# Layer 1's experts: from every expert over all tokens to 23 gathered tiles of one expert each

## Chip, core and metric

The kernel is one program on one core of a Trainium2 chip. The metric is the device time of one execution in microseconds (us), as the median of several runs. Before the change it is 3067.04 us over 3 runs (3048.27 to 3077.75).

## What is computed

The program runs four layers over the same activations `x`, of which the kernel handles two batches of 1024 tokens with 128 channels, all in f32. Each layer normalises `x`, sends the result both through an attention part (giving `s`) and through a feed-forward part (giving `g` before a silu), and adds `s * silu(g)` to `x`. The change is in the feed-forward part of the second layer ("layer 1"), a mixture of eight experts of which each token uses two:

```python
probs = softmax(einsum('bsd,ed->bse', x, Wr))          # 8 experts
topv, topi = top_k(probs, 2)
combine = sum(topv[..., None] * one_hot(topi, 8), axis=2)
for w1, bb1, w2, bb2, ce in experts:                    # w1 128x512, w2 512x128
    h = gelu(x @ w1 + bb1, approximate=False)
    acc = acc + ce[..., None] * (h @ w2 + bb2)
```

An expert that a token did not choose has weight zero in the sum, so the reference's value is the same whether that expert's product is computed for the token or not.

## The kernel before

**How the program is built.** Each layer's two parts are Python generators that write instructions and `yield` now and then. `weave` (L423) interleaves them: in every turn a stream gets its rate added, and it advances one yield for each whole unit. `program` (L1712) calls it for layer 1 with the attention of both batches as one stream at rate 1 and the feed-forward of both batches, one after the other, as a second stream at rate `R1[1]` = 0.125: one feed-forward yield in eight attention yields. When the attention stream is used up, the feed-forward stream goes on alone. The order on each engine is fixed when the program is built. Position in the program is the priority; an instruction that is taken to be ready may be placed ahead of an earlier one that is not, so pieces of one stream also slip into gaps of the other. [...]

**Buffers.** Most data lie in one pool of 33 buffers of 128 x 1048 f32 (`half` and `arr`; `NHALF`), some in eight buffers of 128 x 512 (`t512`). PSUM has four banks for general use (`bank`) and two double banks (`bank2`). The weights of a layer have one buffer for the attention part (`wa`) and one for the feed-forward part (`wf`), which the next layer's weights reuse.

**Layer 1's attention** (`l1_attn`, L768). For each batch, four groups of four heads; for each group 16 rounds of a key tile by a query half. A round is four score products `sim` (into the two double banks), two exponentials `e` of 128x1024 on ACT (L882; each result takes a pool buffer), and the four products `av` of the round before, which accumulate in two of the four general banks over the whole group. One round is one yield; a group has 18 yields, so the two batches have 144. At the end of a batch its output is transposed and projected (`wt`, `pj`).

**Layer 1's feed-forward** (`l1_ffn`, L932). For each batch: eight small router products, a softmax and the rank of every expert for each token on DVE (L942 to L953), the combine weights `comb` (L955), the transposes of these and the product with `b2` that starts the sum `g`; one yield. Then 16 steps, for each expert and each half of 512 tokens: four `up` products (weights 128x128, 512 token columns), a Gelu on ACT from each of them (L977), 16 `down` products (128 tokens by 128 outputs each, four accumulated per token tile), and four DVE instructions that weight the result and add it to `g` (L988); one yield. A batch has 17 yields. `up` weights lie in `wf` (`w1`, 4096 columns), `down` weights in four pool buffers that are loaded ahead of the layer (`w2`, from `f1b`).

After both streams, `step` (L1734 to L1736) applies silu to `g`, multiplies by `s` and adds to `x`, and the next layer normalises `x`.

The trace has two matmul records for each f32 product of the code, one for a transpose. All products have the line of the helper `mm` (L335), all transposes L339; they are told apart by the name of the tile that they write.

Of the kernel before, what the change touches and what calls it, by code (L numbers as in the profile page):

```python
# [16 lines left out]
F32 = mybir.dt.float32  # L17
I32 = mybir.dt.int32
AF = mybir.ActivationFunctionType
ALU = mybir.AluOpType  # L20
X = mybir.AxisListType.X
PSUM = bass.MemoryType.PSUM

P = 128
NB = 2
L = 1024
T = NB * L
NT = T // P
TB = L // P
BLK = 512  # L30
NB2 = L // BLK
# [11 lines left out]
def _cols(v):  # L43

    v = np.asarray(v).reshape(-1)
    n = -(-v.size // P)
    out = np.zeros((n * P,), v.dtype)
    out[: v.size] = v
    return out.reshape(n, P).T


def _chunks(w):

    w = np.asarray(w)
    n = -(-w.shape[0] // P)
    out = np.zeros((n * P, w.shape[1]), w.dtype)
    out[: w.shape[0]] = w
    return out.reshape(n, P, w.shape[1]).transpose(1, 0, 2).reshape(P, -1)
# [12 lines left out]
def _pad(w):  # L71
    w = np.asarray(w)
    out = np.zeros((P, w.shape[1]), w.dtype)
    out[: w.shape[0]] = w
    return out


def _gains(q, k):
# [45 lines left out]
    ],  # L124
    "f1": [
        ("wr", 8, lambda i: i["L1_ffn_Wr"].T),
        ("b1", 32, lambda i: _cols(i["L1_ffn_b1"])),
        ("b2", 128, lambda i: _pad(i["L1_ffn_b2"])),
        ("w1", 4096, lambda i: i["L1_ffn_W1"].transpose(1, 0, 2).reshape(P, -1)),
    ],  # L130
    "a2": [
        ("wk", 1024, lambda i: i["L2_attn_Wk"].reshape(P, -1)),
# [37 lines left out]
        for l in range(2)  # L170
    },
    "f0b": [("h2", 2048, lambda i: _chunks(i["L0_ffn_h2_w"].T))],
    "f1b": [("w2", 4096, lambda i: _chunks(i["L1_ffn_W2"].reshape(-1, P)))],
}


def _constants():

    p = np.arange(P)[:, None]
    c = np.arange(P)[None, :]  # L180
    s = np.arange(192)[None, :]
    one = np.float32(1)
    strict = (c[:, :32] < p % 32) * one
    incl = (p % 32 <= c[:, :32]) * one
    return {
        "ident": (p == c) * one,
        "bo32": (p // 32 == c // 32) * one,
        "strict32": strict,
        "incl32": incl,
        "pad32": ((p // 32 == c[:, :32] % 4) & (p % 32 < 8)) * one,  # L190
        "quad4": (p // 32 == c[:, :4]) * one,
        "row8": (p % 32 == 8) * one,
        "bo64": (p // 64 == c // 64) * one,
        "upper": (p <= c) * one,
        "center": (p == c) * one - one / P,
        "mean": one / P + 0 * (p + c),


        "window": np.concatenate([np.where((s >= p) & (s <= p + 64), 0, -1e30)[:, o:] for o in (128, 0, 0)], axis=1),

        "every2": (c[:, :33] % 2 == 0) * one + 0 * p,
        "every4": (c[:, :35] % 4 == 0) * one + 0 * p,

        "turns": (p // 64 == c[:, :32] % 2) * one,

        "spread": np.concatenate([(p == 32 * (h % 4) + h // 4) * one + 0 * c[:, :64] for h in range(16)], axis=1),

        "spread2": (p % 32 == c // 64) * one,
        "ones": one + 0 * p + 0 * c,
        "head8": (p // 8 == c[:, :16]) * one,  # L210
        "slot": np.where(c < 127, c, -1) + 0 * p,
        "inv4": one / np.float32(10000) ** (np.arange(0, 8, 2, dtype=np.float32) / 8) + 0 * p,
    }


def _rotary():


    f = np.float32
    half = np.arange(0, 64, 2, dtype=f)  # L220
    t = np.arange(L, dtype=f)
    freqs = t[:, None] * (f(1) / f(10000) ** (half / f(64)))[None, :]
    power = (t - f(L // 2)) / f(32)
    scale = ((half + f(0.4 * 64)) / f(1.4 * 64))[None, :] ** power[:, None]
    cos, sin = np.cos(freqs), np.sin(freqs)
    both = [np.concatenate([sign * v, v], axis=1)
            for sign, v in ((1, cos * scale), (1, cos / scale), (-1, sin * scale), (-1, sin / scale))]
    tab = np.concatenate(both, axis=1).astype(f)
    return tab.reshape(TB, P, 256).transpose(1, 0, 2).reshape(P, -1)
# [14 lines left out]
def pack_inputs(inputs):  # L244
    out = {"x": np.ascontiguousarray(inputs["L0_attn_hidden_states"])}
    for name, spec in PACKS.items():
        out[name] = _pack(spec, inputs)
    out["bkv2"] = np.concatenate([np.reshape(inputs[f"L2_attn_b{n}"], (1, -1)) for n in "kv"], axis=1)
    out["mask2"] = np.ascontiguousarray(inputs["L2_ffn_attention_mask"][:NB, 0])

    pos = np.asarray(inputs["L2_ffn_position_ids"])[:NB]
    pos = np.pad(pos, ((0, 0), (0, L - pos.shape[1])), mode="edge")
    out["pos2"] = np.ascontiguousarray(pos.reshape(NT, P).T)

    out["stair"] = (np.arange(2 * L - P)[None, :] - (L - P) < np.arange(P)[:, None]).astype(np.float32)
    out["rotary"] = _rotary()
    out["const"] = np.ascontiguousarray(
        np.concatenate([v.astype(np.float32) for v in _constants().values()], axis=1)
    )
    return out  # L260
# [149 lines left out]
def tiles(v):  # L410
    return v.rearrange("p (t d) -> p t d", d=P)


def cols(t, n=1, w=P):
    return slice(t * w, (t + n) * w)


R0 = (20, 0.3)
R1 = (1, 0.125)
R2 = (1, 0.2, 0.2)  # L420


# [506 lines left out]
    C.project(out["s"], wT, w["wp"], w["bp"])  # L929


def l1_ffn(C, w, xnT, out):  # L932

    nc = C.nc
    E = 8
    n = TB * E
    ps = C.bank("router")
    for t in range(TB):
        C.mm(ps[:, t * E : (t + 1) * E], xnT[:, cols(t)], w["wr"])
    bye = lambda v: v.rearrange("p (t e) -> p t e", e=E)  # L940
    prob = bye(C.small("prob", n))
    nc.vector.tensor_copy(prob, bye(ps[:, :n]))  # L942
    C.softmax(prob, TB, E)

    rank = bye(C.small("rank", n))
    nc.gpsimd.memset(rank, 0.0)
    for f in range(E):
        pf = prob[:, :, f : f + 1]
        for lo, hi, op in ((0, f, ALU.is_gt), (f + 1, E, ALU.is_ge)):
            if lo < hi:  # L950
                c = C.small("cmp", TB * (hi - lo)).rearrange("p (t e) -> p t e", t=TB)
                nc.vector.tensor_tensor(c, pf.to_broadcast([P, TB, hi - lo]), prob[:, :, lo:hi], op)
                nc.vector.tensor_add(rank[:, :, lo:hi], rank[:, :, lo:hi], c)  # L953
    comb = bye(C.small("comb", n))
    nc.vector.scalar_tensor_tensor(comb, rank, 1.5, prob, ALU.is_lt, ALU.mult)  # L955

    acc, cT = C.arr("g"), C.arr("cT")
    for g in range(NB2):
        ps = C.bank("tr")
        for k in range(4):  # L960
            C.transpose(ps[:E, cols(k)], comb[:, 4 * g + k, :])
        C.evac(cT[:E, cols(g, 1, BLK)], ps[:E])
    for g in range(NB2):
        ps = C.bank("b2")
        for k in range(4):
            C.mm(ps[:, cols(k)], cT[:E, cols(4 * g + k)], w["b2"][:E])
        C.evac(acc[:, cols(g, 1, BLK)], ps)
    yield

    for e in range(E):  # L970
        for i in range(NB2):
            hh = [C.arr(f"h{a}") for a in range(2)]
            h = [hh[c // 2][:, cols(c % 2, 1, BLK)] for c in range(4)]
            for c in range(4):
                ps = C.bank("up")
                C.mm(ps, w["w1"][:, e * 512 + c * P : e * 512 + (c + 1) * P], xnT[:, cols(i, 1, BLK)])
                nc.scalar.activation(h[c], ps, AF.Gelu, bias=w["b1"][:, 4 * e + c : 4 * e + c + 1])  # L977
            ps = C.bank("down")
            for k in range(4):
                for c in range(4):  # L980
                    C.mm(
                        ps[:, cols(k)], h[c][:, cols(k)], w["w2"][e // 2][:, cols(4 * (e % 2) + c)],
                        start=c == 0, stop=c == 3,
                    )
            for k in range(4):
                t = 4 * i + k
                a = acc[:, cols(t)]
                nc.vector.scalar_tensor_tensor(a, ps[:, cols(k)], comb[:, t, e : e + 1], a, ALU.mult, ALU.add)  # L988
            yield
    out["g"] = acc  # L990


# [719 lines left out]
def program(tc, ins, out):  # L1712
    with ExitStack() as es:
        C = Ctx(es, tc, ins)
        nc = C.nc
        tokens = lambda d, b: d[b].rearrange("(t p) d -> p t d", p=P)
        x = []
# [24 lines left out]
        def layer(attn, ffn, rates):  # L1742
# [8 lines left out]
        wa, wf = C.weights("a0", "wa"), C.weights("f0", "wf")  # L1751
# [3 lines left out]
            lambda a, f: weave((a[0], 1), (a[1], 1, R0[0]), (chain(*f), R0[1])),  # L1755
        )
        wa, wf = C.weights("a1", "wa"), C.weights("f1", "wf")
        wf["w2"] = [C.loaded(f"w2_{i}", ins["f1b"][:, cols(i, 1, L)]) for i in range(4)]
        layer(
            lambda x, b, r: l1_attn(C, wa, x[1], r), lambda x, b, r: l1_ffn(C, wf, x[1], r),  # L1760
            lambda a, f: weave((chain(*a), R1[0]), (chain(*f), R1[1])),
        )
        wa, wf = C.weights("a2", "wa"), C.weights("f2", "wf")
# [5 lines left out]
        s = l3_attn(C, C.weights("a3", "wa"), xns)  # L1769
# [27 lines left out]
```

## Time and profile before

| | |
|---|---|
| Median of 3 runs | 3067.04 us |
| The profiled execution: its time / its span | 3056.8 us / 3055.0 us |
| Busy over the span: PE, DVE, ACT, POOL | 83%, 43%, 39%, 14% |
| Layer 1: from its first score products to the last sum into `g` | about 667 to 1436 us |
| In 690 to 1310 us (620 us): PE, DVE, ACT, POOL busy | 583.0, 92.6, 400.9, 4.9 us |
| In 1310 to 1440 us (130 us): PE, DVE, ACT, POOL busy | 121.3, 27.1, 53.5, 0.1 us |
| Share of the chain that ended last: PE, DVE, ACT | 62%, 19%, 10% |
| Indirect transfers, or other transfers issued by POOL | none in the program |

An engine's line shows how long its instructions ran. A row of groups or of the timeline has the line of the code, the engine, the tile written and the tiles read, the number of records, and the idle time before them with what ended it. PE records are pipelined and overlap each other: what a product costs is read from the distance between starts, not from a record's length. "Windows" gives each engine's busy time in a stretch of the span.

### The profile page before, as it was taken

The page shows a single profiled execution, that of the slowest core. Times are in us where ns is not written, and L with a number is a line of the kernel's source. Part 1 is how long each engine was busy: PE and PEld are TensorE (multiplying, and loading weights), DVE is VectorE, ACT ScalarE, POOL GpSimd, SP SyncE. Part 2 cuts the span into 40 slices and gives each one's busy share as a digit, 9 for nine tenths or more (in the row PEclk, how much of TensorE's full clock was granted, in tenths as well). Part 3 has the DMA queues.
Part 4 walks back from the last instruction along what each step waited for, and adds up shares of the span by engine and source line. Part 5 has one row for each costly group of instructions (what it writes and reads, how often), then busy time and mean ns, then how long its engine had stood idle before and what let it go on. Part 6 is the DMA issues. An engine that isn't in the chain of part 4 may idle for free.

```text
span 3055.0 us, 32385 instructions
## 1 busy us (share of the span) xinstructions
PE 2547.6 (83%) x13394; PEld 1288.6 (42%) x13394; DVE 1311.4 (43%) x2114; ACT 1180.4 (39%) x1488; POOL 417.9 (14%) x444
## 2 busy tenths in 40 slices
PE   6788975779999999997679687689989968878887
PEld 3445543433333333365335353433334335544554
DVE  4767577342101111023774655431122046566564
ACT  3300112245676766634111212353444424444443
POOL 0000102100000000000111110021111144343330
PEclk8866766788999999999778877799999978999998
DMA  2000000010000000001110000000000000000000
GB/s 85 19 21 15 1 0 1 11 57 1 1 1 1 1 1 1 1 29 57 52 56 21 1 0 24 17 1 1 1 1 1 8 31 1 8 8 1 4 4 8
DMA packets 33941, 41.78 MB, mean 14 GB/s; under 512 B 19969, under 2 KB 24833, under 8 KB 33665
## 3 DMA queue, kind: packets, MB, share of 16 engines
q1 hardware_dynamic: 33792, 39.70, 4.1%
q8 instruction: 105, 1.72, 0.2%
q14 instruction: 44, 0.35, 0.0%
HBM read 36.54 MB, written 3.15 MB: 13 GB/s over the span
## 4 chain that ended last, share of the span: by engine, by line
PE 62%; DVE 19%; ACT 10%; issue 4%; POOL 3%; SPq 1%; DMA 1%; POOLq 0%; ACTq 0%; DVEq 0%
PE sim L335 11%; PE num L335 6%; PE down L335 4%; PE av L335 4%; PE tr L339 3%; PE up L335 3%; PE z L335 3%; PE wo L335 3%; PE nd L335 3%; PE ph L335 2%; PE qk L335 2%; PE step L335 2%; PE spread L335 1%; PE hs L335 1%; PE pu L335 1%
## 5 line engine op out<-in xcount | busy, mean ns | idle before, releaser
L882 ACT ACTIVATE e<-sim 128x1024 f32<-128x1024 f32 x256 | 250.2, 1021 | 139.7 <-PE sim L335 139.4
L335 PE MATMUL sim<-q,k 32*128 32x512 f32 x1024 | 254.1, 674 | 4.4 <-ACT e L882 3.9
L988 DVE SCALAR_TENSOR_TENSOR g<-down,comb,g 128x128 f32<-128x128 f32 x128 | 36.0, 344 | 430.3 <-PE down L335 430.3
L1388 ACT ACTIVATE e<-sim 128x1024 f32<-128x1024 f32 (+1 forms) x192 | 146.8, 809 | 175.0 <-PE sim L335 174.8
L335 PE MATMUL num<-e,v 128*64 128x512 f32 (+4 forms) x1280 | 196.5, 429 | 0.9 <-POOL e L1390 0.9
L335 PE MATMUL sim<-q,kT 64*128 64x512 f32 (+3 forms) x768 | 159.5, 522 | 23.7 <-ACT sq L1348 14.2
L1390 POOL TENSOR_TENSOR e<-e,const 128x256 f32<-128x256 f32 x128 | 85.5, 680 | 530.1 <-ACT e L1388 526.5
L335 PE MATMUL av<-e,va 128*32 128x512 f32 x1024 | 156.8, 633 | 0.0
L332 DVE COPY q<-num 128x512 f32<-128x512 f32 x16 | 11.1, 691 | 323.7 <-PE num L335 323.7
L335 PEld LDWEIGHTS down<-w,h 128*128 128x128 f32 x1024 | 123.5, 193 | 48.9 <-ACT h L977 37.7
L335 PEld LDWEIGHTS sim<-q,k 32*128 32x128 f32 x1024 | 77.2, 193 | 158.2 <-ACT e L882 131.3
L335 PE MATMUL down<-w,h 128*128 128x128 f32 x1024 | 130.3, 280 | 9.0 <-ACT h L977 8.9
L335 PE MATMUL z<-e,const 128*32 128x192 f32 (+5 forms) x1344 | 130.6, 415 | 1.6 <-ACT e L1597 1.6
L335 PE MATMUL up<-xnT,w_f 128*128 128x512 f32 x256 | 123.9, 609 | 2.1 <-ACT h L977 2.0
L1542 POOL TENSOR_TENSOR sq<-qk,tab 128x256 f32<-128x256 f32 x128 | 97.2, 791 | 206.9 <-DVE ss L1531 191.4
L335 PEld LDWEIGHTS num<-e,v 128*64 128x64 f32 x1280 | 81.2, 137 | 94.0 <-issue 72.3
L335 PEld LDWEIGHTS sim<-q,kT 64*128 64x128 f32 x768 | 62.5, 188 | 131.3 <-issue 71.3
L977 ACT ACTIVATE h<-up,w_f 128x512 f32<-128x512 f32 x128 | 85.2, 686 | 72.9 <-PE up L335 71.2
L1014 POOL TENSOR_SCALAR e<-e 128x512 f32<-128x512 f32 x32 | 48.2, 1510 | 302.3 <-ACT e L1013 295.2
L339 PE MATMUL tr<-const,u 128*128 128x128 f32 x384 | 60.8, 316 | 33.7 <-DVE u L1550 29.3
L600 DVE SCALAR_TENSOR_TENSOR conv<-vT,w_a,conv 128x1024 f32<-128x1024 f32 x60 | 81.3, 1355 | 1.4
L335 PE MATMUL g<-z,w_f 128*128 128x512 f32 (+1 forms) x48 | 36.4, 851 | 53.3 <-DVE z L1656 53.3
(506 smaller groups left out, 4572.3 us busy)
## 6 DMA issues: line engine op xcount, KB each, us to landing
stair<-in_stair SPq DMA_DIRECT2D x16, 512.0 KB, 3.6
w_f<-in_f SPq DMA_DIRECT2D x14, 512.0 KB, 5.0
w_a<-in_a SPq DMA_DIRECT2D x8, 512.0 KB, 4.5
w<-in_f1b SPq DMA_DIRECT2D x4, 512.0 KB, 7.5
mk<-in_mask SPq DMA_DIRECT2D x4, 512.0 KB, 5.1
tab<-in_rotary SPq DMA_DIRECT2D x4, 512.0 KB, 3.8
const<-in_const SPq DMA_DIRECT2D x1, 1422.5 KB, 6.0
x<-in_x SPq DMA_DIRECT2D x2, 512.0 KB, 8.0
```

The costliest lines, as they stand in the source:

```text
L332: self.nc.vector.tensor_copy(dst, src)
L335: self.nc.tensor.matmul(out, lhsT=lhsT, rhs=rhs, start=start, stop=stop, **k)
L339: self.nc.tensor.transpose(out, in_, self.ident[:n, :n])
L600: nc.vector.scalar_tensor_tensor(av, vT[:, f + t : f + t + L], cw[:, t : t + 1], av, ALU.mult, ALU.add)
L882: nc.scalar.activation(es[jj], ps[jj].rearrange("p i n -> p (i n)"), AF.Exp)
L977: nc.scalar.activation(h[c], ps, AF.Gelu, bias=w["b1"][:, 4 * e + c : 4 * e + c + 1])
L988: nc.vector.scalar_tensor_tensor(a, ps[:, cols(k)], comb[:, t, e : e + 1], a, ALU.mult, ALU.add)
L1014: nc.gpsimd.tensor_scalar_min(e, e, 1.0)
L1388: nc.scalar.activation(e[:, :, :n], ps[:, :, :n], AF.Exp, scale=16.0)
L1390: nc.gpsimd.tensor_tensor(e[:, :, :P], e[:, :, :P], C.c["upper"].unsqueeze(1).to_broadcast([P, 2, P]), ALU.mult)
L1542: nc.gpsimd.tensor_tensor(t4[:, j, :, a], c4[:, j, :, z], sin, ALU.mult)
```

## The change

The feed-forward part of layer 1 computes each token only with its two experts. A batch has 2048 pairs of token and expert; sorted by expert, with each expert's block filled up to a multiple of 128, they fit into at most 23 tiles of 128 slots whatever the routing, and the program always runs 23. DVE and small products find the slot of each pair, then for each slot its token and weight, and for each tile its expert. POOL issues indirect transfers ("gathers", one row of DRAM per partition by an index in SBUF): per tile one for the 128 tokens (from a copy `xd` of the normalised activations in DRAM) and one for the expert's weights (from a new input `experts`, 1028 f32 to a row: `w1`, `w2` and the bias); and 16 per batch to collect the results by slot from a DRAM copy `yd`. The tiles run in six sets of up to four with a yield after each. The bias is added by a DVE instruction ahead of the Gelu instead of by the Gelu itself. The `b2` product is moved to the end. `w1`, `b1` leave the `f1` pack and the four `w2` loads go. Rate `R1[1]` is 0.2 instead of 0.125.

```diff
-R1 = (1, 0.125)
+R1 = (1, 0.2)
...
-def l1_ffn(C, w, xnT, out):
+def l1_ffn(C, w, xn, xnT, b, out):
...
+    NTILE = (2 * L + E * (P - 1)) // P
+    xd = C.dram.tile([L, P], F32, tag=f"xd{b}", name="xd")
+    nc.sync.dma_start(out=xd.rearrange("(t p) d -> p t d", p=P), in_=tiles(xn))
...
+    yield
+    sel, comb = bye(C.small("sel", n)), bye(C.small("comb", n))
+    nc.vector.tensor_single_scalar(sel, rank, 1.5, ALU.is_lt)
+    nc.vector.tensor_mul(comb, sel, prob)
+    before = C.t512("before")[:, : (TB + 1) * E].rearrange("p (t e) -> p t e", e=E)
+    nc.gpsimd.memset(before[:, 0], 0.0)
+    for t in range(TB):
+        nc.vector.tensor_add(before[:, t + 1], before[:, t], sel[:, t])
+    ps = C.bank("place")
+    C.mm(ps[:, :n], C.c["upper"], sel.rearrange("p t e -> p (t e)"), stop=False)
+    C.mm(ps[:, :n], C.c["ones"], before[:, :TB].rearrange("p t e -> p (t e)"), start=False)
+    C.mm(ps[:, n : n + E], C.c["ones"], before[:, TB])
+    yield
...
+    slots = C.sml.tile([P, 2 * TB], I32, tag="slots", name="slots", bufs=2)
+    nc.vector.tensor_copy(slots, slot)
+    yield
+    rows = [C.arr(f"rows{k}") for k in range(2)]
+    for k in range(2):
+        nc.vector.tensor_tensor(
+            tiles(rows[k]), C.c["count"].unsqueeze(1).to_broadcast([P, TB, P]), over(row[:, k * TB : (k + 1) * TB], P),
+            ALU.is_equal,
+        )
...
+    ps = C.bank("fill")
+    for a in range(2 * TB):
+        C.mm(
+            ps[:, : 2 * NTILE], rows[a // TB][:, cols(a % TB)], put[:, a].rearrange("p s j -> p (s j)"),
+            start=a == 0, stop=a == 2 * TB - 1,
+        )
+    token = C.sml.tile([P, NTILE], I32, tag="token", name="token", bufs=2)
...
+    expert = C.sml.tile([P, NTILE], I32, tag="expert", name="expert", bufs=2)
+    nc.vector.tensor_copy(expert, owner)
+    yield
+    def gather(dst, src, index):
+        nc.gpsimd.indirect_dma_start(
+            out=dst, out_offset=None, in_=src, in_offset=bass.IndirectOffsetOnAxis(ap=index, axis=0)
+        )
+    yd = C.dram.tile([NTILE * P, P], F32, tag=f"yd{b}", name="yd")
+    for j0 in range(0, NTILE, 4):
+        js = range(j0, min(j0 + 4, NTILE))
+        m = len(js) * P
+        xg, y = C.t512("xg"), C.t512("y")
+        for j in js:
+            gather(xg[:, cols(j - j0)], xd, token[:, j : j + 1])
+        ps = C.bank("tr")
+        for j in js:
+            C.transpose(ps[:, cols(j - j0)], xg[:, cols(j - j0)])
+        xT = C.t512("xT")
+        nc.vector.tensor_copy(xT[:, :m], ps[:, :m])
+        hs, ws = [], []
+        for j in js:
+            we = C.half("we")[:, : 2 * 512 + 4]
+            gather(we, C.ins["experts"], expert[:, j : j + 1])
+            ps = C.bank("up")
+            for c in range(4):
+                C.mm(ps[:, cols(c)], we[:, cols(c)], xT[:, cols(j - j0)])
+            h = C.t512("h")
+            nc.vector.tensor_tensor(tiles(h), tiles(ps), over(we[:, 1024:], P), ALU.add)
+            nc.scalar.activation(h, h, AF.Gelu)
+            hs.append(h)
+            ws.append(we)
+        ps = C.bank("down")
+        for j, h, we in zip(js, hs, ws):
+            for c in range(4):
+                C.mm(ps[:, cols(j - j0)], h[:, cols(c)], we[:, 512 + c * P : 512 + (c + 1) * P], start=c == 0, stop=c == 3)
+        nc.vector.tensor_tensor(
+            tiles(y[:, :m]), tiles(ps[:, :m]), over(weight[:, j0 : j0 + len(js)], P), ALU.mult
+        )
+        nc.sync.dma_start(out=yd[j0 * P : j0 * P + m].rearrange("(t p) d -> p t d", p=P), in_=tiles(y[:, :m]))
+        yield
     acc, cT = C.arr("g"), C.arr("cT")
...
-    for e in range(E):
-        for i in range(NB2):
-            hh = [C.arr(f"h{a}") for a in range(2)]
...
-            yield
+    for k in range(2):
+        y = C.arr(f"y{k}")
+        for t in range(TB):
+            gather(y[:, cols(t)], yd, slots[:, k * TB + t : k * TB + t + 1])
+        nc.vector.tensor_add(acc, acc, y)
+        yield
     out["g"] = acc
...
-        wf["w2"] = [C.loaded(f"w2_{i}", ins["f1b"][:, cols(i, 1, L)]) for i in range(4)]
```

## The prediction

> **What bounds the kernel now.** I read the page for the busiest engine and the chain that ended last, then windows over layer 1, then chain and timeline inside it. PE is the busiest engine of the kernel and carries the chain. Windows of layer 1 (columns: us, then busy time and records of PE, PE weight loads, DVE, ACT, POOL, then granted clock), first the stretch with both streams, then the one in which the experts run alone:
>
> ```profile
> PE 62%; DVE 19%; ACT 10%; issue 4%; POOL 3%; SPq 1%; DMA 1%; POOLq 0%; ACTq 0%; DVEq 0%
> ```
>
> ```profile
> 690.00:1310.00 620.00, 582.98 (x2942) 217.61 (x2941) 92.61 (x323) 400.93 (x436) 4.86 (x9) 0.95 0.00 1
> 1310.00:1440.00 130.00, 121.32 (x673) 89.73 (x672) 27.13 (x75) 53.45 (x74) 0.11 (x1) 0.96 0.12 40
> ```
>
> PE is at 94% and 93%. POOL does nothing. Is PE the bound of attention alone, too? Windows over six attention rounds without an expert step (16.01 us), and over eight rounds with one expert step (31.88 us):
>
> ```profile
> 858.04:874.05 16.01, 15.90 (x99) 4.41 (x97) 0.17 (x1) 11.71 (x13) 0.00 (x0) 1.00 0.01 2
> 858.04:889.92 31.88, 31.11 (x180) 11.15 (x177) 1.30 (x5) 24.46 (x26) 0.00 (x0) 1.00 0.00 1
> ```
>
> A round takes 16.01/6 = 2.67 us, PE busy 99%, ACT 73%. An expert step among them takes 31.88 - 8 x 2.67 = 10.5 us. The PE timeline of the tail shows what such a step is when alone:
>
> ```profile
> 1409.35 2.74 PE L335 MATMUL up<-xnT,w_f 128*128 128x512 f32 x6
> 1411.92 0.83 PE L335 MATMUL down<-w,h 128*128 128x128 f32 x6
> 1412.59 1.02 PE L335 MATMUL up<-xnT,w_f 128*128 128x512 f32 x2
> 1413.45 3.06 PE L335 MATMUL down<-w,h 128*128 128x128 f32 x26
> 1416.35 2.74 PE L335 MATMUL up<-xnT,w_f 128*128 128x512 f32 x6
> ```
>
> From 1409.35 to 1416.35 it is 7.0 us with no gap: 8 `up` records at 0.43 us between starts (1412.59 to 1413.45 for two) and 32 `down` records at 0.112 us (1413.45 to 1416.35 for 26). So 3.5 of the 10.5 us among attention are not products. The ACT timeline there shows them: Gelu and exponential take turns with a table load of 1.28 us each.
>
> ```profile
> 879.45 0.69 ACT L977 ACTIVATE h<-up,w_f 128x512 f32<-128x512 f32 x1 [0.64 <-PE up L335]
> 880.16 1.28 ACT L882 ACT_TABLE_LOAD   x1
> 881.45 1.02 ACT L882 ACTIVATE e<-sim 128x1024 f32<-128x1024 f32 x1
> 882.49 1.28 ACT L977 ACT_TABLE_LOAD   x1
> ```
>
> **What the skill says.** The Trainium skill, "DMA: Bandwidth & Descriptors", Anatomy of one DMA — SWDGE (gpsimd) path, prices a transfer issued by POOL at about 2.0 us plus bytes/436e3 us, mostly completion latency. The trace has no such transfer; its loads of 512 KB issued by SP, which the page puts on another path, land in 3.5 to 9 us. Same page, Issuing engines are not separate DMA queues: all issuers share the 16 DMA engines; here they are idle in the stretch (DMA share 0.00 above), so bandwidth is free. "SBUF — State Buffer", Who interferes with whom: a POOL-issued transfer of about 620 ns takes about 3100 ns beside a DVE copy in two-port mode, as POOL cannot write descriptors meanwhile. No run here shows it; DVE is busy only 15% of the stretch.
>
> **Removed.** Each batch has 16 steps. Those of the first lie among attention: 16 x 10.5 = 168 us. Those of the second run alone from 1317.15 us to the last sum at 1436.2: 119 us. Together 287 us, of which 32 x 7.0 = 224 us are products. The 128 Gelus (0.687 us, 88 us of ACT) and 128 sums on DVE (36 us) go with them. At the layer's start, four loads of 512 KB on SP go; they were behind other work and I cost them at nothing (one PSUM copy on ACT waited 3.7 us for them; it may come back).
>
> **Added on PE.** A product of 128 columns is two records, 2 x 0.112 = 0.223 us. A tile has four `up` and four `down` products and one transpose (8 take 1.85 us from 1311.73 to 1313.58: 0.23). That is 8 x 0.223 + 0.23 = 2.01 us; 46 tiles: 92.5 us. The 16 `fill` and 3 `place` products are small; the nearest row is the router's, 16 records in 1.85 us, 0.23 us a product: 19 x 0.23 = 4.4 us a batch, 8.8 us for both. Router, `comb` transposes and `b2` products stay. Sum 101 us: PE's work falls by 123 us, and with products as the bound that is the core of the gain.
>
> **Added waits.** Each of the 12 sets has the path transposes, `xT` copy, `up`, bias add on DVE (0.69 us as other 128x512 rows from PSUM), Gelu 0.69 us, `down`, and the switch of tables there and back. Before, a step lost 3.5 us on that; a set has one more link (DVE) and shorter `up` runs (four products of 0.223 us, not 0.86) to hide it, but attention rounds fill gaps as they did. I take 4.5 us a set: 12 x 4.5 = 54 us. Bounds: 2 us (mostly filled) 24 us; 8 us (tables switched for every tile) 96 us. ACT has room: two loads for each of 46 tiles are 118 us, and it has 620 - 401 us idle there, plus the 56 us of Gelus saved (82 x 0.687).
>
> **Routing on DVE.** About 45 instructions at 0.15 to 0.23 us (the L952 and L953 rows), two of 128x1024 at 1.23 us, and five middle ones, 1.5 us in all: some 12 us a batch. They stand under attention rounds, with four yields between their stages, each 5 x 2.67 = 13 us. Cost nothing; without that cover about 20 us. PE's wait for `comb` (5.58 us in the second batch, 3.1 in the first) goes, as `comb` is used late: gain 9 us, against which I put the first wait for a `fill` or a gather, so zero net. Bias adds (46 x 0.69), `xT` and `y` (24 x 0.69), final sums (4 x 1.23) put 53 us on DVE against 36 taken off.
>
> **Gathers on POOL.** A set of four issues 4 token gathers of 64 KB (2.15 us by the skill's price, an estimate) and 4 weight gathers of 526 KB (3.2 us): 21.4 us even if wholly serial. A set's turn is five rounds, 13.3 us, plus its own 4 x 2.01 + 4.5 = 12.5 us: 25.8 us. So gathers keep ahead if one costs POOL up to 3.2 us on average, and nothing shows on PE. The 16 result gathers (34 us serial) come after the last set; 144 attention yields allow 28 expert yields and there are 24, so 20 rounds, 53 us, are left over them. SP's new stores (`xd`, six `yd`) stand in a queue idle in layer 1; next-layer weights behind them gain, as `wf` is free earlier.
>
> **End of the layer.** The tail goes, so the second batch's output path (`asb`, `wt`, `pj`, from 1297.4) is exposed: about 3 us of waits more. Table load and silu (2.3 us from 1436.24) come off its path, as `g` is early. Net +3 with the last DVE sum.
>
> **Sum.** Cost after: 101 + 54 = 155 us; before 287; gain 132, less 3 and 1 for the larger constants: 128 us. On the profiled execution's span, 3055 - 128 = 2927 us, 2929 as a time. The median of the runs shown stands 10 us above that execution (3067.04 to 3056.8): 2939 us.
>
> **Rivals.** (1) *Gathers set the pace*: PE's list is fixed, so a late gather holds all attention products behind it. Above 3.2 us of POOL per gather, a set grows by 8 x (cost - 3.2); 12 sets give back 128 us at 3.2 + 128/96 = 4.5 us. At 5 us, 173 us are lost: 3112 us, slower. For it: no row of the trace bounds it, and the skill's 3.1 us beside DVE copies is near. Against: the price without them, and DVE's low load. (2) *Partial*: `we` tiles, which can be fetched as soon as a buffer is free, take the pool buffers that `e` needs. In the trace the `va` clearing for the second batch waited 308 us for an `e` buffer, so the pool is full in this layer already; but four `w2` and up to four `h` buffers come free. Starved, a round runs `av`, two exponentials and half of `sim` in line, 1.0 + 2.1 + 0.5 = 3.6 us instead of 2.67. Over half of 128 rounds: +60 us, 2999 us. Or the second batch's results stick out by about 40 us. (3) *No effect*: starved in all 128 rounds, the loss is 122 us and the time 3061 us. Against: PE's gaps in such rounds are where expert products would go, and fetched weights leave the pool as these run. That attention is bound by its exponentials, so that steps only filled gaps, is excluded by PE 99% and ACT 73% in bare rounds; that a skewed routing leaves more work cannot be, as the number of tiles is fixed.
>
> **Chances.** A measurement of this kernel can tell about 1% (31 us) from no change. Forecast, 2890 to 2970: 0.58. Partial, 2970 to 3035: 0.24. No effect: 0.06. Gathers slower than break-even: 0.12. Faster thus 0.82, same 0.06, slower 0.12. The range 2890 to 3035 covers the first two, 0.82; its low end is the sum with 24 us of waits (2909) and the 19 us by which the lowest run before lies under its median.
>
> **What would show it.** Right: layer 1's last sum near 1310 us; no stretch of `up` and `down` alone; POOL with 124 transfers under 3 us each; sets of 8 us of products; bare rounds still 2.67 us. Wrong: PE idle before `tr<-const,xg` or `up<-we` released by a DMA (rival 1); rounds of 3.5 us with ACT waiting for an `e` buffer (rival 2); table loads well over 100 in the layer (waits above 54 us).

## The result, and the profile after

The changed kernel takes 2976.5 us (median of 4 runs, 2964.44 to 2980.08) against 3067.5 us (4 runs) before: ratio 0.9704, 95% interval 0.9648 to 0.9759. It is 91 us faster, where 128 were forecast. The profiled executions say where: span 2975.7 us against 3055.0, a gain of 79.3 us where the sum made for them said 128. I split both spans at layer 1's first `sim` product and at its last sum (the last `g` sum before, the last `s` sum after):

| | before | after | gain | forecast |
|---|---|---|---|---|
| layer 0, up to the first `sim` | 667.2 | 678.9 | -11.7 | 0 |
| layer 1 | 769.0 | 675.6 | 93.4 | 132 |
| the rest | 1618.8 | 1621.3 | -2.5 | -4 |

So layer 1 gave 39 us less than forecast, and layer 0, which the change doesn't touch, lost 12. (Of the 4 us forecast for the rest, 3 were for an output path that falls inside layer 1 as cut here; the split of the forecast between these two rows is loose by that much.) PE still carries the chain; "another core or an unknown queue" is new in it:

```profile
PE 63%; DVE 19%; ACT 7%; issue 5%; POOL 3%; another core or an unknown queue 1%; SPq 1%; DMA 1%; POOLq 0%; ACTq 0%; DVEq 0%
```

Windows of the changed kernel (columns as in the prediction), the stretch with both streams and ten bare attention rounds at the end:

```profile
690.00:1310.00 620.00, 562.44 (x2987) 241.11 (x2989) 145.71 (x428) 349.99 (x382) 122.78 (x136) 0.89 0.19 54
1315.31:1341.65 26.34, 26.34 (x164) 7.55 (x161) 0.00 (x0) 19.40 (x21) 0.11 (x1) 1.00 0.01 1
```

Bare rounds are as before, 26.34/10 = 2.63 us at the full clock. But PE is busy 562 of 620 us instead of 583, and its mean clock fell from 0.95 to 0.89: PE has new gaps, and slow products after them. POOL's groups in layer 1 rule out the rival that gathers set the pace:

```profile
L1054 POOL DMA_INDIRECT xg<-xd,token x46 | 44.0, 956 | 246.5 <-DMA yd<-y 99.5 <-DVE weight L1039 72.6 <-DVE token L1037 58.0
L1054 POOL DMA_INDIRECT we<-in_experts,expert x46 | 43.3, 942 | 73.3 <-PE down L341 29.2 <-ACT e L888 11.8 <-issue 10.0
L1054 POOL DMA_INDIRECT y<-yd,slots x32 | 30.3, 947 | 73.3 <-ACT e L888 39.1 <-PE sim L341 25.3 <-issue 8.5
```

A gather occupies POOL for 0.95 us, with 0.30 us to the next, whether it moves 64 or 526 KB; PE's waits name no gather. What is new shows in ACT's waits in layer 1 (total, times, longest). I quote the two lines for `e`, and that for the copies of `g`:

```profile
ACT e L888 <- PE sim L341: 152.1, 119, 9.6
...
ACT e L888 <- remote: 31.8, 6, 10.6
...
ACT g L336 <- remote: 15.6, 2, 10.8
```

"Remote" is the profile's word for a release that it can put down to no engine or queue of this core. ACT, which before never waited for one in this layer, waited 50.7 us for them (3.3 of these for a `cT` copy). The first of these waits, in ACT's timeline and then PE's:

```profile
770.82 1.02 ACT L888 ACTIVATE e<-sim 128x1024 f32<-128x1024 f32 x1 [0.44 <-PE av L341]
779.31 1.02 ACT L888 ACTIVATE e<-sim 128x1024 f32<-128x1024 f32 x1 [7.46 <-remote]
```

```profile
771.90 1.13 PE L341 MATMUL sim<-q,k 32*128 32x512 f32 x4 [0.34 <-issue]
772.96 1.06 PE L341 MATMUL av<-e,va 128*32 128x512 f32 x8
773.95 0.66 PE L345 MATMUL tr<-const,xg 128*128 128x128 f32 x4
780.38 1.22 PE L341 MATMUL sim<-q,k 32*128 32x512 f32 x2 [5.78 <-issue]
```

The exponential at 779.31 waits only for products of PE and for an earlier instruction of ACT itself, and the pair of `sim` products whose turn it is stands in PE's records before 771.90. It started over 7 us later; DVE's `xT` copy, which waits only for the transposes of 773.95, started at 780.93. PE, whose next product needs that exponential, stood for 5.78 us. POOL was in a run of 13 gathers, from 760.6 to 776.9. There are four large ones of this kind: after 12 or 13 gathers at the start of each batch (780 and 1090 us) and in the 16 gathers that collect each batch's results (955 to 967, and 1260 to 1272). Two shorter ones follow runs of 8 and of 6 gathers: the exponentials at 815.91 and 901.18 waited 4.67 and 2.57 us for a remote release. At 955 to 967 PE stands for 3.76 and 9.52 us. ACT there, then PE's second wait:

```profile
947.95 0.58 ACT L336 COPY cT<-tr 8x512 f32<-8x512 f32 x1 [3.80 <-issue]
953.35 0.59 ACT L336 COPY g<-b 128x512 f32<-128x512 f32 x1 [4.82 <-remote]
953.83 1.03 ACT L888 ACTIVATE e<-sim 128x1024 f32<-128x1024 f32 x1
965.43 1.94 ACT L888 ACTIVATE e<-sim 128x1024 f32<-128x1024 f32 x2 [10.57 <-remote]
```

```profile
966.51 2.08 PE L341 MATMUL sim<-q,k 32*128 32x512 f32 x4 [9.52 <-ACT e L888]
```

I call these stalls. The 16 gathers there run from 942.56 to 962.28 without a pause.

### The profile page after: what moved, and what is told of

Its sections match the earlier page's. It is cut to its first block, busy times and chain, and to the rows that moved or that the text cites. A ratio compares the mean times of both kernels' runs of the same rounds, so it can differ in the third digit from the quotient of the medians.

```text
span 2975.7 us, 31819 instructions
## 1 busy us (share of the span) xinstructions
PE 2448.3 (82%) x12972; PEld 1235.8 (42%) x12972; DVE 1348.6 (45%) x2160; ACT 1102.6 (37%) x1388; POOL 536.4 (18%) x572
## 4 chain that ended last, share of the span: by engine, by line
PE 63%; DVE 19%; ACT 7%; issue 5%; POOL 3%; another core or an unknown queue 1%; SPq 1%; DMA 1%; POOLq 0%; ACTq 0%; DVEq 0%
PE sim L341 13%; PE num L341 6%; PE av L341 5%; PE tr L345 4%; PE z L341 3%; PE wo L341 3%; PE nd L341 3%; PE ph L341 3%; PE down L341 2%; PE up L341 2%; PE qk L341 2%; PE step L341 2%; PE spread L341 2%; PE rh L341 1%; PE pu L341 1%
## 5 line engine op out<-in xcount | busy, mean ns | idle before, releaser
L341 PE MATMUL sim<-q,k 32*128 32x512 f32 x1024 | 264.0, 705 | 34.6 <-ACT e L888 23.6
L341 PE MATMUL av<-e,va 128*32 128x512 f32 x1024 | 170.2, 652 | 0.0
L1054 POOL DMA_INDIRECT xg<-xd,token x46 | 44.0, 956 | 246.5 <-DMA yd<-y 99.5
L341 PE MATMUL g<-z,w_f 128*128 128x512 f32 (+1 forms) x48 | 36.3, 848 | 53.3 <-DVE z L1776 53.3
L341 PEld LDWEIGHTS z<-e,const 128*32 128x32 f32 x1344 | 43.9, 108 | 79.6 <-issue 67.4
L1663 POOL TENSOR_TENSOR u<-u,sq 128x1024 f32<-128x1024 f32 x32 | 76.1, 2378 | 2.5
L341 PE MATMUL ph<-h,w_h 128*128 128x512 f32 x128 | 70.2, 690 | 6.7 <-ACT h L763 4.2
L1653 DVE TENSOR_TENSOR u<-qk,tab 128x1024 f32<-128x1024 f32 x32 | 44.0, 1376 | 67.9 <-ACT qk L1649 44.2
```

The source lines that it names most:

```text
L341: self.nc.tensor.matmul(out, lhsT=lhsT, rhs=rhs, start=start, stop=stop, **k)
L1054: nc.gpsimd.indirect_dma_start(out=dst, out_offset=None, in_=src, in_offset=bass.IndirectOffsetOnAxis(ap=index, axis=0))
L1653: nc.vector.tensor_tensor(split(u), split(c), self.tab[:, k, 0].unsqueeze(2).to_broadcast([P, 2, H, DH]), ALU.mult,)
L1663: nc.gpsimd.tensor_tensor(u, u, sq, ALU.add)
```

## Experiments

All start from the changed kernel. "Layer 1" is taken from each profile as above; it is steadier than the time, which has layer 0's 12 us in it. "Remote" is what ACT waited for remote releases in layer 1. The runs come from four chips, on which the kernel before takes 3058.9 to 3059.9 us (medians); the chip of the changed kernel's own runs is not on record. A ratio is to the kernel before on the same chip.

| | chip | median us | ratio to before, interval | layer 1 | remote |
|---|---|---|---|---|---|
| changed kernel | not on record | 2976.5 | 0.9648 to 0.9759 | 675.6 | 50.7 |
| the same again (e5) | 11 | 2967.8 | 0.9666 to 0.9760 | 678.7 | 53.3 |
| rate 0.125 (e1) | 1 | 2948.5 | 0.9563 to 0.9694 | 644.6 | none |
| rate 0.16 (e6) | 11 | 2965.3 | 0.9644 to 0.9738 | 668.7 | 29.4 |
| rate 0.25 (e7) | 11 | 2976.6 | 0.9694 to 0.9787 | 672.4 | 31.1 |
| no experts (e2) | 1 | 2779.7 | 0.9029 to 0.9143 | 484.9 | none |
| plain collection on SP (e3) | 1 | 2914.6 | 0.9452 to 0.9559 | 611.5 | none |
| only the collection on POOL (e8) | 11 | 2929.6 | 0.9537 to 0.9622 | 628.1 | 10.5 |
| all transfers plain on SP (e4) | 1 | 2904.0 | 0.9417 to 0.9523 | 604.8 | none |
| sums on POOL (e9) | 7 | 2969.2 | 0.9624 to 0.9733 | 673.8 | 32.0 |
| and paced sets (e10) | 7 | 2944.5 | 0.9553 to 0.9655 | 652.0 | 13.4 |
| and the collection in fours (e11) | 4 | 2931.7 | 0.9501 to 0.9621 | 632.0 | none |
| plain collection on POOL (e12) | 4 | 2935.0 | 0.9522 to 0.9623 | 644.3 | 16.0 |

### e1: the rate undone

```diff
-R1 = (1, 0.2)
+R1 = (1, 0.125)
```

> The changed kernel with one part of the change undone: the feed-forward rate is 0.125 again instead of 0.2. The two batches have 24 feed-forward yields; 144 attention yields now let 18 of them in, so the second batch's last sets and its collection come after the attention. Theory (hiding is part of the gain, as the prediction's 'tail' term has it): four sets of 8 us of products with little to fill their waits, then the collection of 16 transfers of 1.25 us and its landing, stand alone, some 65 us, while the attention ends some 45 us earlier: 2990 to 3010 us. Rival (the rate is worth nothing, since about 80 us of attention rounds run bare at the end of the changed kernel anyway): within 8 us of 2976.

2948.5 us, and the profile has the tail that I expected: the attention ends at 1243.1 us and the last `g` sum at 1309.2, 66 us later. Yet the kernel isn't slower, for layer 1 is 31 us shorter than with rate 0.2 and has no stall. Theory and rival are both wrong on the time. That the lower rate took the stalls away is not shown: e1 ran on chip 1, where rate 0.2 was not run, and its own runs of 12 and 13 gathers beside the attention pass without a stall. The collection of the first batch is broken here into two runs of 8 gathers, 12 us apart.

### e2: no experts

The lines from the slots to the last expert set, the collection and the store of `xd` are taken out.

> Leaves out all of the experts of layer 1 (slots, transfers, up, Gelu, down, collection); only the router, the rank and the product with b2 remain, so the sum g is only that product. It prices what experts cost in the kernel before and in the changed one, as the time of either less this one. If the prediction's removed term (287 us) was right and the cost of the new experts (155 us) too small: 3067 - 287 = 2780 us, and the new experts cost 196 us. If the new cost was right and the removed term too large: 2976 - 155 = 2821 us, and the old experts cost 246 us. Between these, both were off.

2779.7 us, the first of the two numbers. Windows over its layer 1:

```profile
666.57:1151.47 484.90, 462.36 (x2417) 142.08 (x2416) 82.53 (x285) 301.50 (x334) 4.97 (x10) 0.95 0.01 3
```

The old experts cost 769.0 - 484.9 = 284 us (forecast 287), the new ones 675.6 - 484.9 = 191 us (forecast 155). What fails is the price of the new ones.

### e3, e8 and e4: which transfers cost

In e3 the collection is `nc.sync.dma_start(out=tiles(y), in_=yd[k * L : (k + 1) * L].rearrange(...))`; in e8 the token and weight transfers are plain instead, as below; e4 has both.

```diff
-            gather(xg[:, cols(j - j0)], xd, token[:, j : j + 1])
+            r = j % TB
+            nc.sync.dma_start(out=xg[:, cols(j - j0)], in_=xd[r * P : (r + 1) * P])
...
-            gather(we, C.ins["experts"], expert[:, j : j + 1])
+            r = j % E
+            nc.sync.dma_start(out=we, in_=C.ins["experts"][r * P : (r + 1) * P])
```

> The changed kernel, but the 16 indirect transfers per batch that collect results by slot are replaced by two plain loads of 512 KB on SP of rows 0 to 2047 of the result copy, so results reach the wrong tokens (the collection by slot is left out). Theory A (a run of twelve or more POOL-issued transfers in a row holds up ACT, DVE and PE): the two idle stretches of PE of 9 to 13 us near 950 and 1257 us of the span, which stand inside or after the 16 transfers, go, those after the first transfers of each batch stay: 20 to 30 us less, 2946 to 2956. Rival B (they come from what the list waits for, such as the landing of the stores of yd, whoever fetches them): the stretches stay, 2970 to 2980.

> As the one before, and the token and weight transfers too are plain loads on SP (64 KB and 526 KB each, of fixed tokens and a fixed expert for each tile), so the routing is computed but not followed. No POOL-issued transfer is left; as many bytes move, by the other path. Theory A (runs of POOL-issued transfers hold the other engines): all four idle stretches go, some 33 us of idle time and part of the half clock that follows each, 2930 to 2945 us. Rival B (the bytes or the landing are what counts, not who issues): the stretches after the first weights of each batch stay, within 8 us of the run with plain collection alone. Rival C (the prediction's waits were too small and the transfers are innocent): within 10 us of 2976.

> The counterpart of the run with plain collection: the 16 transfers per batch that collect results stay indirect on POOL, while token and weight transfers are plain loads on SP of fixed tokens and a fixed expert for each tile (the routing is computed but not followed). Theory A (the collection is what costs, 62 us by the earlier pair): 2955 to 2970 us. Rival B (the cost needs both kinds on POOL): 2900 to 2920 us.

e3 took 62 us off, more than theory A asked, and *all* stalls went, also those that A left in place. e4, at 2904.0, is below A's 2930 to 2945; as it moves the same bytes, its rivals B and C are out. e8 fell between its two cases. By layer 1: the token and weight gathers alone (e3 less e4) cost 611.5 - 604.8 = 6.7 us, the collection alone (e8 less e4) 23.3 us, and both together 70.8 us.

That seems to leave 41 us which belong to neither kind alone, but the 6.7 us are from chip 1, where these gathers pass without a stall. In e12 (chip 4, below) the same gathers stall beside contiguous transfers for the collection, and layer 1 is 644.3 - 604.8 = 39.5 us above e4. On chip 11, making them plain (e8 against e5) takes off 678.7 - 628.1 = 50.6 us. With 39.5 and 23.3 us little is left over for both kinds together. The plain loads also no longer wait for the routing's results, which no run here tests apart. Windows over layer 1 of the changed kernel and of e4:

```profile
678.87:1354.44 675.57, 614.86 (x3275) 257.61 (x3274) 154.49 (x457) 386.74 (x422) 122.89 (x137) 0.90 0.17 50
666.31:1271.06 604.75, 583.29 (x3275) 245.12 (x3274) 154.23 (x457) 385.65 (x422) 5.20 (x13) 0.95 0.17 55
```

PE's idle time in e4 is 604.75 - 583.29 = 21.5 us, against 22.5 us in e2 without experts: with plain transfers the sets' table loads, DVE links and routing cost nothing beyond PE's own busy time of 583.3 - 462.4 = 121 us. Of the 70.8 us, 39.2 are idle PE (60.7 - 21.5) and 31.6 busy PE, at a mean clock of 0.90 where e4 has 0.95.

### e5, e6 and e7: again, and other rates

> The changed kernel itself, profiled a second time. The run with plain collection has the same instructions in the same order up to the first collection, yet PE had no idle stretch after the first weights there, where the changed kernel lost 20 us between its 40th and 56th exponential. Theory (a property of the one profiled execution, which differs from one to the next): the idle stretches stand elsewhere or are missing in this profile, and the median is anywhere between 2950 and 2980. Rival (a property of the program): idle stretches of 4 to 10 us at the same four places, 2970 to 2980.

> The changed kernel with the feed-forward rate 0.16 instead of 0.2: 144 attention yields let 23 of the 24 feed-forward yields in, so only the end of the collection stands after the attention. Theory (the rate 0.2 itself costs something, as 0.125 was 28 us faster with a tail of 65 us): with the collisions of 0.2 gone and no tail, 2895 to 2925 us. Rival (the gain of 0.125 lay in attention that is less starved, in proportion to the rate): between the two, 2950 to 2975.

> The changed kernel with rate 0.25: the experts run still closer and end some 30 attention rounds before the attention does. Theory (the cost at 0.2 is bound to where the collections fall among the attention): no ordered answer, anywhere from 2920 to 2990, with idle stretches only where a collection meets rounds that wait for a buffer. Rival (density of transfers is the cost): more idle time than at 0.2, 2985 to 3010.

e5 has its idle stretches at the same four places of the program, and all 256 exponentials of its layer 1 come within 4 us of the first's: the stalls are not one execution's, and my theory there is wrong, though the median is 2 us below the rival's range and inside the theory's. At 0.16 stalls of 5.5 and 5.2 us follow the 12 gathers at the start of each batch, and the second collection (16 gathers) stands at the end of the layer, so that layer 1 is only 10 us shorter than e5's on the same chip: the rival's range, though not by its reason. At 0.25 PE stands 11.2 us at the first collection; the time doesn't grow with the rate, so density of transfers is not the rule.

### e9, e10 and e11: breaking the runs

e9 lets POOL add what it has collected, e10 adds a copy on POOL that waits for the set's transposes, e11 collects into one small target. e11's edits (e9 keeps the two targets of 1024 columns; e10 is e9 and the `pace` line):

```diff
         nc.vector.tensor_copy(xT[:, :m], ps[:, :m])
+        nc.gpsimd.tensor_copy(C.small("pace", 1), xT[:, :1])
...
+    y = C.arr("y")[:, :BLK]
     for k in range(2):
-        y = C.arr(f"y{k}")
-        for t in range(TB):
-            gather(y[:, cols(t)], yd, slots[:, k * TB + t : k * TB + t + 1])
-        nc.vector.tensor_add(acc, acc, y)
+        for h in range(NB2):
+            for t in range(4 * h, 4 * h + 4):
+                gather(y[:, cols(t % 4)], yd, slots[:, k * TB + t : k * TB + t + 1])
+            s = cols(h, 1, BLK)
+            nc.gpsimd.tensor_tensor(acc[:, s], acc[:, s], y, ALU.add)
```

> The changed kernel, but POOL adds the collected results to g itself, 128 x 512 at a time, instead of two adds of 128 x 1024 on DVE. Nothing else moves and nothing is left out. POOL must wait for what it has fetched, so the 16 transfers of a batch come in two runs of 8 with a pause between, not in one run of 16. Theory (a run of twelve or more POOL-issued transfers without a pause is followed by 3 to 10 us in which ACT, DVE and PE stand, while runs of up to 8 are not): the idle stretches at the two collections go and those after the first transfers of each batch stay; 30 to 45 us less than the changed kernel, 2925 to 2940 us. Rival (the collection is dear for what it holds or when it ends, not for its runs): the sums on POOL end later, so 2965 to 2985 us.

> As the one before, and in each set POOL also copies one column of the turned tokens xT into a spare tile, so that it has to wait for that set's transposes between the set's weight transfers. That breaks the run of 12 or 13 at the start of each batch as well. Theory of runs: all four idle stretches go and the time comes near the kernel whose loads are all plain (2904): 2905 to 2925 us. Rival (the stretch after the first weights comes from the bytes of 8 weight transfers, 4 MB, not from the run): it stays, within 8 us of the run before. Second rival (fetching ahead was needed): weights come late, PE waits for we, slower than the run before.

> As the paced run, but the collection has one target of 128 x 512 instead of two of 128 x 1024, so that POOL has to add each four transfers before it fetches the next four: runs of 4 with pauses of 2 to 4 us. Nothing is left out. In the paced run a stretch of 3.7 us stayed at the first collection, in which ACT, DVE and PE stood from the sixth transfer of a run of 8 to 1 us after its last. Theory (the stall begins some six to eight transfers into a run): it goes, and so does most of the 27 us by which the two collections were still longer than with plain loads; 2920 to 2932 us. Rival (what stays is the price of fetching on POOL at all, or of sums that end later): 2940 to 2955 us.

e9 missed: of the 3.7 and 9.5 us at the first collection only the 9.5 went, the second collection kept its stalls, and the time is in the rival's range. A run of 8 is still long enough to stall, so "twelve or more" was wrong, as the changed kernel's two short stalls say too. e10 did what the theory says at the start of each batch: both stalls there are gone, with the same gathers and bytes; layer 1 is 22 us shorter. The second rival's waits came with it (12.1 us of PE for weights), but the run is faster all the same. It stays above its range, and what stalls are left stand at the collections, still in runs of 8. The token and weight gathers of e10 and e11 come in runs of 5 to 8 and do not stall, so the length alone is not the rule. In e11 POOL's timeline shows the collection in fours:

```profile
928.27 0.96 POOL L1054 DMA_INDIRECT y<-yd,slots  x1 [12.74 <-PE sim L341]
929.53 0.95 POOL L1054 DMA_INDIRECT y<-yd,slots  x1 [0.30 <-issue]
930.79 0.94 POOL L1054 DMA_INDIRECT y<-yd,slots  x1 [0.30 <-DMA y<-yd,slots]
932.04 0.94 POOL L1054 DMA_INDIRECT y<-yd,slots  x1 [0.30 <-issue]
936.14 1.26 POOL L1111 TENSOR_TENSOR g<-g,y 128x512 f32<-128x512 f32 x1 [3.15 <-ACT g L336]
937.67 0.96 POOL L1054 DMA_INDIRECT y<-yd,slots  x1 [0.27 <-POOL g L1111]
```

No wait of ACT's in layer 1 is put down to a remote release any more, no stall is left, and the clock is back (0.94). Windows over its layer 1:

```profile
680.66:1312.64 631.98, 595.21 (x3275) 251.34 (x3274) 150.07 (x453) 386.33 (x422) 135.29 (x157) 0.94 0.18 53
```

e11 computes everything and beats both kernels: 2931.7 us, its interval below that of the changed kernel. Layer 1 is 44 us shorter than there and still 27 us longer than with plain transfers; 12.2 us of that are waits of PE for weights, which the changed kernel has not and the pacing makes late:

```profile
PE up L341 <- DMA we<-in_experts,expert: 12.2, 13, 1.5
```

### e12: contiguous transfers on POOL

```diff
-            gather(y[:, cols(t)], yd, slots[:, k * TB + t : k * TB + t + 1])
+            r = k * TB + t
+            nc.gpsimd.dma_start(out=y[:, cols(t)], in_=yd[r * P : (r + 1) * P])
```

> The changed kernel, but the 16 transfers per batch that collect results are contiguous transfers of 64 KB each, still issued by POOL one after the other (rows 0 to 2047 of the result copy, so the collection by slot is left out, as in the run with plain loads on SP). Theory A (what matters is that [...]POOL works 0.95 us on each): a contiguous one is lighter for POOL, the idle stretches at the collections go and so does that after the first weights; 2912 to 2925 us, as with plain loads on SP. Rival B (any run of 16 POOL-issued transfers does it): the four stretches stay, 2960 to 2980 us.

2935.0 us, between the two. The trace says why. POOL is through 8 contiguous transfers in 4.3 us, where 8 gathers take 10 us, and there is no stall at the collections. Those after the first weights of each batch stay (3.52 and 2.65 us of idle PE). So eight contiguous transfers on POOL do not stall where eight gathers did (e9 and e10, on another chip). Whether that is for their kind or for the shorter time on POOL is not separated.

### What the runs leave open

Shown: the stalls stand in or just after runs of POOL's gathers. On chip 11 those at the start of the batches go when token and weight transfers are plain (e8 against e5, 50.6 us of layer 1); on chip 7 they go when these runs are broken, with the same gathers and bytes (e10 against e9, 21.8 us). That a collection in fours has none rests on one kernel, e11, on a chip where e12 has stalls.

A rival is left: the chip. e1 (runs of 12 and 13 gathers beside attention rounds) and e3 (two runs of 16) are the only kernels with such long runs and no stall, and both ran on chip 1, where the changed kernel was not repeated. Up to the first collection e3's instructions are the changed kernel's in the same order. The traces differ in one more way. Engines release each other by semaphores, counters that an instruction raises when it is done. In every other profile with token and weight gathers, 31 to 64 such raises by ACT and DVE have no record (49 in the changed kernel's); in e1 and e3 it is 2 and 3. So whether e1 and e3 were spared by their programs or by their chip stays open, and with it what the rate and the collection cost by themselves.

Not shown: by what path. The trace keeps when semaphores were raised. The one that PE's products raise was raised at 779.23 and at 965.35 us, each time 0.08 us before the waiting exponential started, the usual distance (the median over layer 1 is 0.08 us). So ACT lost no time after the raise; the raise came late, 8.4 us after the end of PE's last record in the second case. But the ends of PE's records are modelled, and the Trainium skill ("Perfetto Trace Analysis", Summary: the profiler window per engine type) too lists TensorE's as an estimated end, so whether PE finished late or only its raise was late can't be told.

## Why the prediction was right in sign and short in size

The time fell just inside the partial case, but by none of the ways that it named: bare rounds are 2.63 us, and only one exponential waited for the `av` products that free an `e` buffer, 0.44 us.

| step, in us of layer 1 | forecast | measured | from |
|---|---|---|---|
| old experts removed | 287 | 284 | before less e2 |
| products added | 101 | 121 | PE busy, e4 less e2 |
| waits of the sets | 54 | 0 | 119.9 - 120.9 |
| gathers, collection included | 0 | 71 | changed kernel less e4 |
| new experts in all | 155 | 191 | changed kernel less e2 |

- **Removed.** The two-part sum (16 steps of 10.5 us among attention, the tail as a whole) holds to 1%: by e2 the first part is 650.9 - 484.9 = 166 us (168 forecast) and the second 118 (119). There is luck in the first: the window of eight rounds from which 10.5 us was read holds nine sets of `av` products, so that one step took 9.5 us, but the sixteen average 10.4.
- **Products.** Two terms were small. The 32 `fill` records of the first batch take 7.06 us in e4, at half clock (0.50) soon after a gap of PE, where I had 16 x 0.23 = 3.7 us; those of the second take 3.77 at full clock. `up` and `down` together are 94 us busy, where 46 x 8 x 0.223 = 82 were expected.
- **Waits of the sets.** "I take 4.5 us a set" was wrong on the safe side, even its low end of 2 us: attention rounds fill the links entirely. Table loads were fewer than feared, 57 in layer 1 against 74 before, where over 100 would have shown the forecast wrong.
- **Gathers, the step that failed.** "Gathers keep ahead [...] and nothing shows on PE", and "20 rounds, 53 us, are left over them" for the collection. The price of a gather was too high, if anything (1.25 us from one to the next where I took 2.15 to 3.2; no run shows the 3.1 us beside DVE copies, whose figures stand in "SBUF — State Buffer" under A bandwidth-pool intuition that's wrong, not in the section that I named), and PE waited for none. I asked only whether gathers come in time. The term that I put at nothing measured 71 us, more than half of the gain forecast: stalls of the other engines in and after runs of gathers, and slower products after them.
- **Rivals.** Starved in all 128 rounds would cost 128 x 0.93 = 119 us, not 122; it did not come.
- **Routing on DVE** at nothing: confirmed by e4's idle time, equal to e2's.
- **End of the layer**: -2.5 us against -4. But the last sum came at 1354 us, not near 1310, as the stalls pushed the attention itself back; the experts were through at 1274.
- **Layer 0.** The 11.7 us aren't the change's. The instructions of PE and ACT there are the same in the same order, but PE's pairs of `rh` products ran at half clock throughout. PE's timeline, before and after:

```profile
535.86 1.11 PE L335 MATMUL rh<-fT,w_a 56*112 56x512 f32 x2
536.90 1.13 PE L335 MATMUL rh<-xnT,w_a 128*128 128x512 f32 x2
```

```profile
536.89 2.07 PE L341 MATMUL rh<-fT,w_a 56*128 56x512 f32 x2
538.89 2.05 PE L341 MATMUL rh<-xnT,w_a 128*112 128x512 f32 x2
```

In the 14 profiles of this study the first `sim` starts at 658 to 668 us eleven times and at 679 to 681 us three times (the changed kernel, e3, e11); in e5, the changed kernel again, it is 658. It is a matter of the execution, and it is in the scatter of the medians.

The forecast gain of 128 us less 79.3 is 48.7: 36 from the new experts, 3 from the old ones, 12 from layer 0, and -1.5 from the rest. Two wrong terms of opposite sign, 54 us of waits that did not come and 71 us of stalls that nobody had, hid each other in the total.

## What to carry to other kernels

Ask of a stream of indirect transfers not only whether it keeps ahead, but how long its runs are and who works beside them: here runs of 12 to 16 were broken into at most 8, and those of the collections into four, by work on the issuing engine that has to wait for what it fetched, and the time was 45 us lower. Compare runs from one chip before a difference is put down to the program: two runs that seemed to settle what the rate and the collection cost came from a chip on which no run of gathers stalled. And take a part out altogether to learn what it costs: two runs (no experts; all transfers plain) showed which terms of the sum were wrong while the total looked nearly right.

## What the runs showed of the hardware that I had not expected

- A gather of 128 rows costs POOL 0.95 us and 0.30 us to the next, for rows of 512 or of 4112 bytes; 8 contiguous transfers of 64 KB take POOL 4.3 us.
- In or after runs of 6 to 16 gathers ACT and DVE stood still although what they wait for had been recorded as done, and PE with them, for 2.0 us (changed kernel) to 11.2 us (e7). On chip 1, in e1 and e3, runs of up to 16 went by without that.
- PE ran at half clock for over 20 us while busy all the time. The Trainium skill ("TensorE: Matmul & The Clock Gate", What's actually happening) has the full clock come back after some 3.4 us of sustained work. Before, it did (full pace from 532.7 us, 5 us after the idle time ended at 527.6); in the changed kernel's execution it did not, and there the measurement stands against the page: PE was busy for 25.66 of 26 us at a clock of 0.50. Windows over that stretch:

```profile
529.00:555.00 26.00, 25.66 (x33) 7.21 (x34) 0.96 (x4) 5.38 (x8) 0.00 (x0) 0.50 0.00 0
```
